# Token order 8p + n in the end stage, with the second channel half scaled and shifted by products on TensorE

## Chip, cores and metric

The kernel runs on one core of one Trainium2 chip. The metric is the device time of a launch in microseconds; the time of a kernel is the median of its runs. All data are fp32.

## The reference

A batch of 16 graphs with 1024 nodes (tokens) and 256 channels passes two layers. Each ends with a residual and a layernorm over the channels:

```
x1 = layernorm(x  + attention(x, adj, ...))                    # layer 0
h  = relu(batchnorm((A_hat @ x1) @ W1.T + b1))                 # layer 1, 512 features
o  = batchnorm(h @ W2.T + b2)        # per channel: o * scale + shift, over all 16 x 1024 tokens
y  = layernorm(x1 + o)
```

The second batchnorm needs statistics over all tokens of all graphs. Its scale and shift are thus known only when the last graph's product with W2 is done, and everything after that point is the end stage.

## The kernel before

The work has four stages. Attention takes the 16 graphs one after the other (until about 1440 us), with the normalised x1 of each graph stored to device memory. The second stage aggregates x1 with the adjacency and applies W1 (until about 2150 us). The third normalises h and applies W2 (until about 2350 us), leaving `o2T[b]`: for each graph b a tile of 128 channels x 2 halves x 1024 tokens, channels on the partitions. The fourth is the end stage.

The instructions of TensorE (PE), ScalarE (ACT) and VectorE (DVE) run in the order in which the program writes them; a scheduler doesn't move them. GpSimd (POOL) also runs in order. SyncE (SP) issues most transfers; the stores of x1 in attention are issued by POOL, in `finish_x1` and, for the last graph, in the second stage.

In memory a graph's x1 is kept as the tile lies on chip: `x1_d[b]` has for each partition p a run of 8 KB, which holds the tokens p, 128 + p, 256 + p and so on. It is written so, read so by `load_x1l` for the second stage, and read so by `load_x1` for the end stage. The output is in plain token order, so the store of `y` breaks into pieces of one token, 1 KB each.

The end stage works graph by graph, in a loop over b that runs `residual2(b)`, then `scale_shift(b + 3)`, then `finish(b - 1)`:

- `scale_shift(b)` applies the batchnorm's scale `sg2` and shift `sh2` to `o2T[b]` in place on ACT, one instruction for each half of 128 channels. Scale and shift are one value for each partition here.
- `residual2(b)` turns `o2T[b]` so that tokens lie on the partitions, in blocks of 128 tokens; two blocks (a "pair") share a bank of PSUM. Pairs 0 and 1 go to two banks `pf`, and DVE adds x1 (`xf[b]`) to them and takes statistics. Pairs 2 and 3 go to the two banks of `held[b]`; there PE itself adds x1, by a product with the identity (`add_x1`), and DVE only takes statistics. `coefficients` makes the layernorm's factors from these, on POOL for nearly all graphs.
- `finish(b)` applies the factors chunk by chunk (a chunk is 128 tokens x 256 channels). Four chunks come from the held banks, four from `xf[b]`. ACT takes six and DVE two; for every third graph ACT takes five and DVE three; for the last graph DVE takes six. The result overwrites `o2T[b]` and is stored by SP. Then a later graph's x1 is loaded.

For graph 0 the eight transposing products into the held banks are written as plain products with the identity, since x1 was put there before:

```
nc.tensor.matmul(
    dst, src, ident, start=(b > 0 and j == c == 0), stop=(b == 0),
    is_transpose=(b > 0), skip_group_check=True,
)
```

The pools of PSUM: two banks for `pf`, and three tiles of two banks for `held`. In attention, bursts of scores and outputs are written out in a fixed order, 16 bursts for each graph; the normalised x1 of the graph before is applied and stored in bursts 2 to 4, and the x of a later graph is loaded in burst 5, into the buffer that the store frees.

Of the kernel before, what the change touches and what calls it, by code (L numbers as in the profile page):

```python
# [10 lines left out]
F32 = mybir.dt.float32  # L11
I32 = mybir.dt.int32
AF = mybir.ActivationFunctionType
ALU = mybir.AluOpType
# [4 lines left out]
P = 128  # L19
# [496 lines left out]
def fast_path(  # L516
# [49 lines left out]
    def tile_o(name):  # L566
        return psum["o"].tile([P, HALF], F32, tag="o", name=name)

    x1_d = [dram.tile([P, NCH, C], F32, tag=f"x1_{b}", name=f"x1_{b}") for b in range(B)]
    c_d = [dram.tile([1, N], F32, tag=f"c_{b}", name=f"c_{b}") for b in range(B)]  # L570
    dinv_d = dram.tile([1, N], F32, tag="dinv", name="dinv")
    den_d = [dram.tile([H, HALF], F32, tag=f"den_{g}", name=f"den_{g}") for g in range(2 * B)]
# [160 lines left out]
    with (  # L733
# [432 lines left out]
        def finish_x1(b, ns=range(NCH)):  # L1166
            st[b]["ln"][1](ns)
            if NCH - 1 in ns:
                nc.gpsimd.dma_start(x1_d[b], st.pop(b)["x"])

        def run(fs, k):
            for f, a in fs[:k]:
# [105 lines left out]

        def load_x1l(b):
            x1l[b] = xp.tile([P, NCH, C], F32, tag="x", name=f"x1l_{b}")  # L1280
            nc.sync.dma_start(x1l[b], x1_d[b])

        agg = {}

# [225 lines left out]
    with (  # L1510
# [123 lines left out]
        for b in range(1, B):  # L1634
            if 1 < b < B - 1:
                load_x1l(b + 1)
                x1_sums(b + 1)
            elif b == B - 1:
                h0 = []
                for i in range(2):  # L1640
                    t = xp.tile([P, 2, N], F32, tag="x", name=f"hl_0_{i}")
                    nc.sync.dma_start(t, h_d[0][:, 2 * i : 2 * i + 2, :])
                    h0 += [t[:, 0, :], t[:, 1, :]]
            steps = aggregate(b)
            for i, step in enumerate(steps):
                step()
                if i == len(steps) - 1 and b < B - 1:
                    later = linear1(b)
                if b > 1 or i > 0:
                    run_linear(lin, 3 if b == 1 and i in (3, 5) else 2)  # L1650
                if b == 1 and i == 0:
                    last_apply()
                    nc.gpsimd.dma_start(x1_d[B - 1], x_last)
                    load_x1l(2)
                    x1_sums(2)
            lin = later
            if b == 1:
                denominators_range()
            if b == 2:
                denominators_good()  # L1660
# [39 lines left out]
    with tc.tile_pool(name="hl", bufs=4) as hl, tc.tile_pool(name="o2p", bufs=1) as o2p:  # L1700
# [5 lines left out]

        def load_x1(b, pool, tag):
            xf[b] = pool.tile([P, NCH, C], F32, tag=tag, name=f"xf_{b}")
            nc.sync.dma_start(xf[b], x1_d[b])

        coefficients2, sg2, sh2 = batchnorm(bn2_st, cols["g2"], cols["be2"], CC, "bn2", nc.vector)
        hs_of = {0: h0}
# [70 lines left out]
                bn2_st[:, c, 2 * b + half, :], o2T[b][:, c, half * HALF : (half + 1) * HALF]  # L1783
            )

        def scale_shift(b, cs=range(CC)):
            for c in cs:
                for hs in (H0, H1) if b == 0 else (slice(0, N),):
                    o = o2T[b][:, c, hs]
                    nc.scalar.activation(  # L1790
                        o, o, AF.Identity, bias=sh2[:, c : c + 1], scale=sg2[:, c : c + 1]
                    )

        load_h(1)
        rest = []
        for b in range(B):
# [63 lines left out]
            for c in range(CC):  # L1860
                last = b == B - 1 and c == CC - 1
                if b:
                    for k, hs in (
                        [(k, hs) for hs in (H0, H1) for k in range(HC)] if last
                        else [(k, hs) for k in range(HC) for hs in (H0, H1)]
                    ):
                        mm(c, k, hs)
                if last:
                    for hs in (H0, H1):
                        nc.scalar.activation(  # L1870
                            o2T[b][:, c, hs], half_ps(c, hs), AF.Identity,
                            bias=cols["b2"][:, c : c + 1],
                        )
                        if hs == H0:
                            scale_shift(0, (0,))
                else:
                    nc.vector.tensor_scalar(
                        o2T[b][:, c, :], pss[c], cols["b2"][:, c : c + 1], None, ALU.add
                    )
                for half, hs in enumerate((H0, H1)):  # L1880
                    nc.vector.bn_stats(bn2_st[:, c, 2 * b + half, :], o2T[b][:, c, hs])
                if b == B - 1:
                    coefficients2(c)
# [8 lines left out]
        with (  # L1892
# [5 lines left out]

            held = {}

            def add_x1(b, pair):
                if b not in held:
                    held[b] = ps_held.tile([P, N], F32, tag="held", name=f"held_{b}")
                nc.tensor.matmul(
                    held[b][:, (pair - 2) * HALF : (pair - 1) * HALF], ident,
                    xf[b][:, 2 * pair : 2 * pair + 2, :].rearrange("p n c -> p (n c)"),
                    start=(b == 0), stop=(b > 0), skip_group_check=True,
                )

            def residual2(b):  # L1910
                xt = xf[b]
                last = b == B - 1
                st = small.tile([P, NCH, 6], F32, tag="ln_st", name=f"st_l1_{b}")
                for pair in range(2):
                    pt = ps_sum.tile([P, HALF], F32, tag="sum", name=f"pf_{b}_{pair}")
                    for j in range(2):
                        n = 2 * pair + j
                        for c in range(CC):
                            nc.tensor.transpose(
                                pt[:, j * C + c * P : j * C + (c + 1) * P],  # L1920
                                o2T[b][:, c, n * P : (n + 1) * P], ident,
                            )
                    xs = xt[:, 2 * pair : 2 * pair + 2, :].rearrange("p n c -> p (n c)")
                    nc.vector.tensor_add(xs, pt, xs)
                    for n in (2 * pair, 2 * pair + 1):
                        nc.vector.bn_stats(st[:, n, :], xt[:, n, :])
                if last:
                    first = coefficients(b, st, M0, nc.vector)
                if b:
                    held[b] = ps_held.tile([P, N], F32, tag="held", name=f"held_{b}")  # L1930
                for pair in range(2, 4):
                    pt = held[b][:, (pair - 2) * HALF : (pair - 1) * HALF]
                    for j in range(2):
                        n = 2 * pair + j
                        for c in range(CC):
                            dst = pt[:, j * C + c * P : j * C + (c + 1) * P]
                            src = o2T[b][:, c, n * P : (n + 1) * P]
                            nc.tensor.matmul(
                                dst, src, ident, start=(b > 0 and j == c == 0), stop=(b == 0),
                                is_transpose=(b > 0), skip_group_check=True,  # L1940
                            )
                    if b:
                        add_x1(b, pair)
                for n in range(4, NCH):
                    nc.vector.bn_stats(st[:, n, :], held[b][:, (n - 4) * C : (n - 3) * C])
                if last:
# [21 lines left out]
            def finish(b, *coeffs):  # L1968
                xt, hx = xf.pop(b), held.pop(b)
                y = o2T[b].rearrange("p c n -> p (c n)").rearrange("p (n c) -> p n c", c=C)  # L1970
                last = b == B - 1
                third = b % 3 == 1
                for n in (0, 1, 2, 3, 6, 7) if last else (0, 1, 2) if third else (0, 1):
                    rstd, nmr = coeffs[n // 4]
                    nc.vector.tensor_scalar(
                        y[:, n, :], hx[:, (n - 4) * C : (n - 3) * C] if n >= 4 else xt[:, n, :],
                        rstd[:, n : n + 1], nmr[:, n : n + 1], ALU.mult, ALU.add,
                    )
                for n in (4, 5) if last else (4, 5, 6, 7, 3) if third else (4, 5, 6, 7, 2, 3):
                    rstd, nmr = coeffs[n // 4]  # L1980
                    nc.scalar.activation(
                        y[:, n, :], hx[:, (n - 4) * C : (n - 3) * C] if n >= 4 else xt[:, n, :],
                        AF.Identity, bias=nmr[:, n : n + 1], scale=rstd[:, n : n + 1],
                    )
                dst = out[b].rearrange("(n p) c -> p n c", p=P)
                if last:
                    nc.sync.dma_start(dst[:, M0, :], y[:, M0, :])
                    nc.scalar.dma_start(dst[:, 4:6, :], y[:, 4:6, :])
                    nc.sync.dma_start(dst[:, 6:8, :], y[:, 6:8, :])
                elif b >= B - 4:  # L1990
# [7 lines left out]
            add_x1(0, 2)  # L1998
            add_x1(0, 3)
            for b in range(1, 4):  # L2000
                scale_shift(b, (0,))
            for b in range(2):
                scale_shift(b, (1,))
            coeffs = {}
            for b in range(B):
                coeffs[b] = residual2(b)
                if b == 0:
                    scale_shift(2, (1,))
                    scale_shift(3, (1,))
                elif b + 3 < B:  # L2010
                    scale_shift(b + 3)
                if b:
                    finish(b - 1, *coeffs.pop(b - 1))
# [44 lines left out]
```

## Time and profile before

| | us |
|---|---|
| median of 3 runs (2448.04 to 2448.85) | 2448.72 |
| the profiled execution: its own time | 2446.23 |
| its span in the profile | 2444.4 |
| PE busy / DVE busy / ACT busy / POOL busy | 2399.5 / 1865.7 / 1234.9 / 476.4 |
| end stage, from the last product with W2 to the end of the span | about 2350 to 2444 |
| last activation starts / last store is issued | 2438.95 / 2439.54 |
| bytes moved by the DMA engines over the span | 221.97 MB, mean 91 GB/s |

The span is the time from the first to the last instruction that the profiler recorded on the core; the run's own time is 1.8 us longer. "Busy" is the sum over an engine's instructions. A matmul's length in the profile includes its drain, which overlaps the next one, so the distance between starts tells the rate. A plain fp32 product leaves two MATMUL records.

### The profile page before, as it was taken

How to read it: one execution, taken by the hardware profiler on the slowest of the kernel's cores; microseconds unless marked ns; L12 is line 12 of the kernel's file. 1: busy time of each engine (PE TensorE's matmuls, PEld its weight loads, DVE VectorE, ACT ScalarE, POOL GpSimd, SP SyncE). 2: the span in 40 equal slices, each digit the busy share in tenths (PEclk: the TensorE clock that was granted, in tenths of full speed). 3: DMA queues.
4: the chain of work that ended last, by engine and by line, in shares of the span. 5: the costliest groups of instructions: out<-in, count | busy, mean ns of one | idle time of the engine just before them, and what ended most of it. 6: DMA issues, size and time to landing. Idle time of an engine off the chain costs nothing.

```text
span 2444.4 us, 32579 instructions
## 1 busy us (share of the span) xinstructions
PE 2399.5 (98%) x12302; PEld 1011.3 (41%) x12302; DVE 1865.7 (76%) x2577; ACT 1234.9 (51%) x1538; POOL 476.4 (19%) x486
## 2 busy tenths in 40 slices
PE   9999999999999999999999999999999999999986
PEld 5343443443434434434344343344444444444443
DVE  5688878878888788788888888956556566479978
ACT  7376675765765756657647667421111111045567
POOL 0021112111311211122112112422122122010026
PEclk9999999999999999999999999999999999999998
DMA  5124232332231332322322327221222222165569
GB/s 164 40 41 86 57 49 70 70 53 67 39 83 53 49 84 56 53 70 54 65 61 44 83 49 96 83 103 69 96 94 77 95 86 86 69 239 174 172 215 337
DMA packets 423190, 221.97 MB, mean 91 GB/s; under 512 B 361584, under 2 KB 394864, under 8 KB 414576
## 3 DMA queue, kind: packets, MB, share of 16 engines
q1 hardware_dynamic: 417920, 169.20, 28.3%
q0 software_dynamic: 4832, 50.34, 4.9%
q8 instruction: 98, 1.61, 0.3%
q14 instruction: 68, 0.56, 0.1%
q10 hardware_dynamic: 272, 0.26, 0.0%
HBM read 136.06 MB, written 83.69 MB: 90 GB/s over the span
## 4 chain that ended last, share of the span: by engine, by line
PE 86%; DVE 9%; ACT 3%; DMA 1%; issue 1%; POOL 0%; POOLq 0%; DVEq 0%; ACTq 0%
PE ps L1051 18%; PE po L1072 18%; PE pgb L883 7%; PE b_agg L1556 4%; PE pga L883 4%; PE c_agg L1556 4%; PE pk L980 4%; PE b_o L1763 3%; PE pv L993 3%; PE a_agg L1556 2%; PE b_h L1588 2%; PE pgc L883 2%; PE pgd L883 2%; PE c_o L1763 2%; PE a_o L1763 2%; PE c_h L1588 2%
## 5 line engine op out<-in xcount | busy, mean ns | idle before, releaser
L1056 ACT ACTIVATE p<-ps 128x1024 f32<-128x1024 f32 x512 | 497.5, 1021 | 183.7 <-PE ps L1051 130.1
L1082 DVE TENSOR_TENSOR acc<-acc,p 128x1024 f32<-128x1024 f32 x384 | 500.1, 1302 | 54.2 <-ACT p L1056 29.3
L1051 PE MATMUL ps<-qT,kT 64*64 64x512 f32 x4096 | 488.1, 592 | 0.3 <-ACT p L1056 0.3
L1072 PE MATMUL po<-p,v 64*64 64x512 f32 x4096 | 485.3, 589 | 0.0
L1147 POOL TENSOR_TENSOR o<-o,r_all 128x512 f32<-128x512 f32 x62 | 94.8, 1538 | 1091.1 <-DVE r_all L1141 1014.5
L1072 PEld LDWEIGHTS po<-p,v 64*64 64x64 f32 x4096 | 158.1, 133 | 281.4 <-issue 274.4
L1051 PEld LDWEIGHTS ps<-qT,kT 64*64 64x64 f32 x4096 | 151.4, 133 | 286.9 <-issue 249.2
L834 DVE SCALAR_TENSOR_TENSOR wg<-wg,adj_s 128x1024 f32<-128x1024 f32 x128 | 149.5, 1216 | 16.5 <-ACT wg L830 16.5
L825 ACT ACTIVATE wg<-crow,ccol 128x1024 f32<-128x1024 f32 x128 | 146.8, 1147 | 0.4 <-DMA crow<-c 0.4
L830 ACT ACTIVATE wg<-wg 128x1024 f32<-128x1024 f32 x128 | 136.0, 1062 | 0.9
L980 PE MATMUL pk<-xT,kvw_s 128*128 128x512 f32 x256 | 121.9, 598 | 3.1 <-ACT drow L1126 3.1
L993 PE MATMUL pv<-kvw_s,xT 128*128 128x256 f32 x512 | 124.0, 385 | 0.0
L993 PEld LDWEIGHTS pv<-kvw_s,xT 128*128 128x128 f32 x512 | 94.9, 190 | 50.0 <-issue 13.4
L893 ACT ACTIVATE qT<-qT 128x512 f32<-128x512 f32 x60 | 37.1, 626 | 149.8 <-DVE qT L896 145.3
L883 PE MATMUL pgb<-wg,S 128*128 128x512 f32 x240 | 111.0, 605 | 0.0
L883 PE MATMUL pga<-wg,x 128*128 128x512 f32 x240 | 109.6, 599 | 0.7 <-ACT qT L906 0.7
L1556 PE MATMUL a_agg<-ahT,x1l 128*128 128x512 f32 x240 | 108.1, 593 | 0.7 <-ACT agg L1298 0.7
L1148 POOL TENSOR_TENSOR x<-x,o 128x512 f32<-128x512 f32 x62 | 107.7, 1748 | 2.4
L1556 PE MATMUL b_agg<-aT,x1S 128*128 128x512 f32 x240 | 107.9, 592 | 0.0
L654 ACT COPY p_agg<-a_agg 128x512 f32<-128x512 f32 x15 | 8.8, 587 | 183.4 <-PE a_agg L1556 183.4
L690 POOL TENSOR_TENSOR x1S<-x1l 128x512 f32<-128x512 f32 x15 | 18.9, 1263 | 352.3 <-PE c_agg L1556 349.0
L1080 DVE TENSOR_TENSOR acc<-p,p 128x1024 f32<-128x1024 f32 x64 | 77.3, 1208 | 7.5 <-ACT p L1056 7.5
(231 smaller groups left out, 3477.1 us busy)
## 6 DMA issues: line engine op xcount, KB each, us to landing
h<-hw POOLq DMA_DIRECT2D x16, 2048.0 KB, 6.7
hl<-h SPq DMA_DIRECT2D x32, 1024.0 KB
x<-x POOLq DMA_DIRECT2D x16, 1024.0 KB, 4.2
x1l<-x SPq DMA_DIRECT2D x16, 1024.0 KB
xf<-x SPq DMA_DIRECT2D x16, 1024.0 KB
o<-oS SPq DMA_DIRECT2D x62, 256.0 KB
o<-o SPq DMA_DIRECT2D x248, 64.0 KB
x<-in_x_dram SPq DMA_DIRECT2D x15, 1024.0 KB
```

The lines of the kernel that those rows point to most:

```text
L825: nc.scalar.activation(w, s["crow"], AF.Abs, bias=s["ccol"][:, n : n + 1])
L830: nc.scalar.activation(w, w, AF.Tanh, scale=0.5)
L834: nc.vector.scalar_tensor_tensor(w, w, 1.0, adj_s[:, n, :], op0=ALU.subtract, op1=ALU.mult)
L883: nc.tensor.matmul(ps, left, right, start=(start and i == 0), stop=(i == NCH // 2 - 1), skip_group_check=True,)
L980: nc.tensor.matmul(ps, kvw_s[:, c, kc * P : (kc + 1) * P], s["xT"][:, c, hs], start=(c == 0), stop=(c == CC - 1),)
L993: nc.tensor.matmul(pt[:, j * C : (j + 1) * C], s["xT"][:, c, n * P : (n + 1) * P], kvw_s[:, c, C : 2 * C], start=(c == 0), stop=(c == CC - 1),
L1051: nc.tensor.matmul(ps[kh * D : (kh + 1) * D, hd * HALF : (hd + 1) * HALF], kT[r, pr, ks], qT[r, pr, qh * HALF : (qh + 1) * HALF], start=Tr ...
L1056: nc.scalar.activation(p, ps, AF.Exp)
L1072: nc.tensor.matmul(g["po"][kh][hd * D : (hd + 1) * D, :], s["v"][r, m, h * D : (h + 1) * D], p[r, hd * HALF : (hd + 1) * HALF], start=(m = ...
L1082: nc.vector.tensor_add(g["acc"], g["acc"], p)
L1556: nc.tensor.matmul(ps, left, right, start=(start and i == 0), stop=(i == NCH // 2 - 1), skip_group_check=True,)
L1763: nc.tensor.matmul(ps, left, right, start=(start and i == 0), stop=(i == 1), skip_group_check=True,)
```

## The change

1. x1 is stored in plain token order: `x1_d[b]` is 1024 x 256. The store in attention and the load for the second stage go through the view `x1_chunks`, with pieces of 1 KB. The store is issued by ACT's queue where POOL issued it.
2. The end stage reads x1 through the view `x1_runs`: partition p holds the tokens 8p to 8p + 7, a run of 8 KB. The output is stored in the same way. The blocks of tokens for the turn are therefore every eighth column, `o2T[b][:, c, n::8]`.
3. ACT scales and shifts only the first 128 channels. For the second 128, the product that turns a block has the diagonal matrix of the scales (`side[:, 0]`) in the identity's place, and a further product of each bank adds the shift (`side[:, 1]` holds the shift of channel k in all columns of row k, and is multiplied with the identity, repeated for both blocks).
4. Order: `back_first` (first half's transposes, and for pairs 2 and 3 the addition of x1) and `back_second` (second half's products) replace the loops of transposes. For graph 0 all four `back_first` are issued ahead.
5. `finish` gives DVE one chunk and ACT seven; for the last graph four each. Where before the last four graphs' outputs were stored in parts, the last two are now, the last one as halves.

The core of the diff:

```diff
-    x1_d = [dram.tile([P, NCH, C], F32, tag=f"x1_{b}", name=f"x1_{b}") for b in range(B)]
+    x1_d = [dram.tile([N, C], F32, tag=f"x1_{b}", name=f"x1_{b}") for b in range(B)]
+    x1_chunks = [d.rearrange("(n p) c -> p n c", p=P) for d in x1_d]
+    x1_runs = [d.rearrange("(p n) c -> p n c", n=NCH) for d in x1_d]
...
-                nc.gpsimd.dma_start(x1_d[b], st.pop(b)["x"])
+                nc.scalar.dma_start(x1_chunks[b], st.pop(b)["x"])
...
-            nc.sync.dma_start(x1l[b], x1_d[b])
+            nc.sync.dma_start(x1l[b], x1_chunks[b])
...
-                    nc.gpsimd.dma_start(x1_d[B - 1], x_last)
+                    nc.scalar.dma_start(x1_chunks[B - 1], x_last)
...
-            nc.sync.dma_start(xf[b], x1_d[b])
+            nc.sync.dma_start(xf[b], x1_runs[b])
...
-        def scale_shift(b, cs=range(CC)):
...
+        def scale_shift(b):
+            o = o2T[b][:, 0, :]
+            nc.scalar.activation(o, o, AF.Identity, bias=sh2[:, 0:1], scale=sg2[:, 0:1])
+
+        side = o2p.tile([P, 2, P], F32, name="side")
...
+            def back_first(b, pair, ps):
+                for j in range(2):
+                    n = 2 * pair + j
+                    nc.tensor.matmul(
+                        ps[:, j * C : j * C + P], o2T[b][:, 0, n::NCH], ident,
+                        start=(j == 0), stop=False, is_transpose=True, skip_group_check=True,
+                    )
+                if pair > 1:
+                    nc.tensor.matmul(
+                        ps, ident, xf[b][:, 2 * pair : 2 * pair + 2, :].rearrange("p n c -> p (n c)"),
+                        start=False, stop=False, skip_group_check=True,
+                    )
+
+            def back_second(b, pair, ps):
+                for j in range(2):
+                    n = 2 * pair + j
+                    nc.tensor.matmul(
+                        ps[:, j * C + P : (j + 1) * C], o2T[b][:, 1, n::NCH], side[:, 0, :],
+                        start=False, stop=False, skip_group_check=True,
+                    )
                 nc.tensor.matmul(
+                    ps.rearrange("p (j c) -> p j c", j=2)[:, :, C1], side[:, 1, :],
+                    ident.unsqueeze(1).to_broadcast([P, 2, P]),
+                    start=False, stop=True, skip_group_check=True,
                 )
...
-                for n in (0, 1, 2, 3, 6, 7) if last else (0, 1, 2) if third else (0, 1):
+                for n in (0, 1, 2, 3) if last else (0,):
...
-                for n in (4, 5) if last else (4, 5, 6, 7, 3) if third else (4, 5, 6, 7, 2, 3):
+                for n in (4, 5, 6, 7) if last else (4, 5, 6, 7, 1, 2, 3):
...
-                dst = out[b].rearrange("(n p) c -> p n c", p=P)
+                dst = out[b].rearrange("(p n) c -> p n c", n=NCH)
...
+            nc.vector.tensor_scalar(side[:, 0, :], ident, sg2[:, 1:2], None, ALU.mult)
+            nc.vector.tensor_scalar(side[:, 1, :], ident, 0.0, sh2[:, 1:2], ALU.mult, ALU.add)
```

More of the change, by code (lines that the diff above doesn't have):

```diff
@@ L1784, in statistics2 @@
             )
-        def scale_shift(b, cs=range(CC)):
[L1787 to L1792, printed above, removed]
+        def scale_shift(b):
+            o = o2T[b][:, 0, :]
+            nc.scalar.activation(o, o, AF.Identity, bias=sh2[:, 0:1], scale=sg2[:, 0:1])
+        side = o2p.tile([P, 2, P], F32, name="side")
         load_h(1)
@@ L1874, in fast_path @@
                         if hs == H0:
-                            scale_shift(0, (0,))
+                            scale_shift(0)
                 else:
@@ L1899, in fast_path @@
             held = {}
-            def add_x1(b, pair):
-                if b not in held:
-                    held[b] = ps_held.tile([P, N], F32, tag="held", name=f"held_{b}")
+            def back_first(b, pair, ps):
[17 more added lines that the diff above has]
+                    )
                 nc.tensor.matmul(
-                    held[b][:, (pair - 2) * HALF : (pair - 1) * HALF], ident,
-                    xf[b][:, 2 * pair : 2 * pair + 2, :].rearrange("p n c -> p (n c)"),
-                    start=(b == 0), stop=(b > 0), skip_group_check=True,
+                    ps.rearrange("p (j c) -> p j c", j=2)[:, :, C1], side[:, 1, :],
+                    ident.unsqueeze(1).to_broadcast([P, 2, P]),
+                    start=False, stop=True, skip_group_check=True,
                 )
@@ L1913, in residual2 @@
                 st = small.tile([P, NCH, 6], F32, tag="ln_st", name=f"st_l1_{b}")
-                for pair in range(2):
[L1915 to L1922, printed above, removed]
+                pts = [ps_sum.tile([P, HALF], F32, tag="sum", name=f"pf_{b}_{pair}") for pair in range(2)]
+                held[b] = ps_held.tile([P, N], F32, tag="held", name=f"held_{b}")
+                pts += [held[b][:, H0], held[b][:, H1]]
+                if b == 0:
+                    for pair in range(4):
+                        back_first(b, pair, pts[pair])
+                for pair in range(2):
+                    pt = pts[pair]
+                    if b:
+                        back_first(b, pair, pt)
+                    back_second(b, pair, pt)
                     xs = xt[:, 2 * pair : 2 * pair + 2, :].rearrange("p n c -> p (n c)")
@@ L1928, in residual2 @@
                     first = coefficients(b, st, M0, nc.vector)
-                if b:
-                    held[b] = ps_held.tile([P, N], F32, tag="held", name=f"held_{b}")
                 for pair in range(2, 4):
[L1932 to L1941, printed above, removed]
                     if b:
-                        add_x1(b, pair)
+                        back_first(b, pair, pts[pair])
+                    back_second(b, pair, pts[pair])
                 for n in range(4, NCH):
@@ L1971, in finish @@
                 last = b == B - 1
-                third = b % 3 == 1
-                for n in (0, 1, 2, 3, 6, 7) if last else (0, 1, 2) if third else (0, 1):
+                for n in (0, 1, 2, 3) if last else (0,):
                     rstd, nmr = coeffs[n // 4]
                     nc.vector.tensor_scalar(
-                        y[:, n, :], hx[:, (n - 4) * C : (n - 3) * C] if n >= 4 else xt[:, n, :],
-                        rstd[:, n : n + 1], nmr[:, n : n + 1], ALU.mult, ALU.add,
+                        y[:, n, :], xt[:, n, :], rstd[:, n : n + 1], nmr[:, n : n + 1],
+                        ALU.mult, ALU.add,
                     )
-                for n in (4, 5) if last else (4, 5, 6, 7, 3) if third else (4, 5, 6, 7, 2, 3):
+                for n in (4, 5, 6, 7) if last else (4, 5, 6, 7, 1, 2, 3):
                     rstd, nmr = coeffs[n // 4]
@@ L1984, in finish @@
                     )
-                dst = out[b].rearrange("(n p) c -> p n c", p=P)
+                dst = out[b].rearrange("(p n) c -> p n c", n=NCH)
                 if last:
                     nc.sync.dma_start(dst[:, M0, :], y[:, M0, :])
-                    nc.scalar.dma_start(dst[:, 4:6, :], y[:, 4:6, :])
-                    nc.sync.dma_start(dst[:, 6:8, :], y[:, 6:8, :])
-                elif b >= B - 4:
+                    nc.scalar.dma_start(dst[:, M1, :], y[:, M1, :])
+                elif b >= B - 2:
                     nc.sync.dma_start(dst[:, M1, :], y[:, M1, :])
@@ L1996, in finish @@
                     load_x1(b + 7, *((hl, "hl") if 3 <= b < 7 else (xp, "x")))
-            add_x1(0, 2)
-            add_x1(0, 3)
             for b in range(1, 4):
-                scale_shift(b, (0,))
-            for b in range(2):
-                scale_shift(b, (1,))
+                scale_shift(b)
+            nc.vector.tensor_scalar(side[:, 0, :], ident, sg2[:, 1:2], None, ALU.mult)
+            nc.vector.tensor_scalar(side[:, 1, :], ident, 0.0, sh2[:, 1:2], ALU.mult, ALU.add)
             coeffs = {}
@@ L2006, in fast_path @@
                 coeffs[b] = residual2(b)
[L2007 to L2010, printed above, removed]
+                if b and b + 3 < B:
                     scale_shift(b + 3)
```

## The prediction

> **What bounds the kernel now.** I read the page first: TensorE (PE) holds 86% of the chain that ended last, and the 40 slices show it saturated until the last two. The changed end stage lies in those two, so I cut that stretch (the answer of busy time by stretch; columns: stretch, its length, then busy us and instructions of PE, PEld, DVE, ACT and POOL, granted clock, DMA share, GB/s).
>
> ```profile
> 2385.00:2390.00 5.00, 3.85 (x21) 2.32 (x20) 4.93 (x14) 5.00 (x9) 3.72 (x11) 1.00 1.06 393
> 2400.00:2405.00 5.00, 3.86 (x21) 2.32 (x20) 4.93 (x13) 5.00 (x9) 3.72 (x12) 1.00 1.05 403
> 2425.00:2430.00 5.00, 3.51 (x19) 1.92 (x17) 4.93 (x15) 3.17 (x7) 3.87 (x11) 1.00 0.75 257
> ```
>
> Here VectorE (DVE) and ScalarE (ACT) are both full, the DMA engines too, and PE has slack. The waits of 2350 to 2445 us say who holds whom:
>
> ```profile
> PEld pf L1919 <- DVE xf L1924: 27.8, 28, 1.2
> PE pf L1919 <- DVE xf L1924: 12.0, 19, 0.7
> POOL w_l L1956 <- DVE st_l L1945: 9.0, 12, 1.8
> ACT o L1981 <- POOL w_l L1965: 8.7, 6, 2.5
> ```
>
> No row of PE, DVE or ACT waits for a DMA: the full DMA engines are nobody's releaser. PE waits for DVE to empty the `pf` banks. The chain in order of time (start, length, what) gives one batch:
>
> ```profile
> 2390.20 0.61 DVE xf L1924
> ...
> 2390.83 0.75 DVE st_l L1926 x2
> 2391.59 0.60 DVE xf L1924
> ...
> 2392.55 0.41 DVE st_l L1926
> 2392.96 1.33 DVE st_l L1945 x4
> 2394.29 0.64 DVE o L1975 x2
> 2394.93 0.61 DVE xf L1924
> ```
>
> From add to add: 4.73 us with two applied chunks; with three, 5.05. From batch 1's first add (2361.18) to batch 14's (2423.95) the mean is 62.77 / 13 = 4.83 us. ACT needs about as much: by the timeline two scale-and-shift start 2.27 us before what follows, four chunks from PSUM take 1.79, two from SBUF 0.99, so 5.05.
>
> PE's prices, from the timeline (start, length with drain, what). Starts, not lengths, give the rate:
>
> ```profile
> 50.86 1.89 PE L993 MATMUL pv<-kvw_s,xT 128*128 128x256 f32 x8
> 52.59 1.88 PE L980 MATMUL pk<-xT,kvw_s 128*128 128x512 f32 x4
> 2356.18 1.95 PE L1938 MATMUL held<-ident,o 128*128 128x128 f32 x16
> 2363.71 0.60 PE L1938 MATMUL held<-ident,o 128*128 128x128 f32 x4
> 2364.15 1.02 PE L1904 MATMUL held<-xf,ident 128*128 128x512 f32 x2
> 2365.01 0.60 PE L1938 MATMUL held<-ident,o 128*128 128x128 f32 x4
> ```
>
> The third row is batch 0, where eight transposing products are written as plain products: 16 records, two for each product, while a true transpose (fourth row, four of them) leaves one. So per record: 128 columns 0.11 us (0.44 / 4 for transposes; (1.95 - 0.27) / 15 = 0.112 for plain ones), 256 columns 1.73 / 8 = 0.216, 512 columns 0.86 / 2 = 0.43. A transpose costs 0.11, a plain 128-column product 0.22, a 256-column one 0.43, a 512-column one 0.86. PE today: 16 transposes and two 512-column adds of x1 per batch, 1.76 + 1.72 = 3.5 us of the 4.83.
>
> **What the Trainium skill says.** "FP8 and Floating Point Precision", TensorE Precision Notes: a true fp32 product takes four passes. "TensorE: Matmul & The Clock Gate", Wait — 56ns, not 53.3ns?: 128 columns take about 56 ns a pass and 512 about 216 when warm. The trace agrees: 0.86 us is four times 216 ns, and the transpose's 0.11 is two passes. "SBUF — State Buffer", Door 1: The DMA port swizzle, has a note on 16-byte lines: an access that crosses to a new line each time pays a penalty, of no stated size. No instruction of PE in this trace reads at such a stride, so nothing here shows it.
>
> **The change part by part.**
>
> *PE, end stage.* Per batch it removes the 8 transposes of channels 128 to 255, and adds 8 plain products with `side` (each 128 columns, 0.22 to 0.23) and 4 shift products (one for each bank, 256 columns, 0.43). Kept: 8 transposes, and two x1 adds. Sum: 8 x 0.11 + 8 x 0.224 + 4 x 0.43 + 2 x 0.86 = 0.88 + 1.79 + 1.72 + 1.72 = 6.1 us. That is 2.6 us more than PE now does and 1.3 more than the present 4.83 us period. PE becomes the bound of the stage.
>
> *DVE and ACT.* DVE applies one chunk a batch in place of two or three: 4.73 - 0.32 = 4.41 us. ACT loses one scale-and-shift (1.14) and applies seven chunks: 1.14 + 1.79 + 3 x 0.49 = 4.4. Both then lie under PE's 6.1, so their relief is worth nothing; its cover is PE. Building `side` is two small DVE instructions (about 0.25 us each, between the 0.15 of the one-column row and the 0.40 of L1975) after the last coefficient, done near 2354.9.
>
> *Start.* Now PE waits till 2355.36 for ACT to scale batch 0's second half. Afterwards it needs only `side`; batch 0's transposes and x1 adds (2.6 us) run before, in PE's idle 2352 to 2355. Start about 2355.05, 0.3 us earlier. Batch 0 then has 4 x (0.45 + 0.43) = 3.5 us of PE left, and 15 batches x 6.1 = 91.7 follow: PE's last bank is full at 2450.3.
>
> *Tail.* The four statistics of the held banks wait for both banks, 1.45 us; coefficients on DVE 1.0 (2434.32 to 2435.31 today); POOL's power and two products 1.9; then ACT alone applies four chunks, 2.0 with the handover, and issues at about +6.6 us. Today ACT's issue at 2439.54 is followed by 4.9 us to the end; the last transfer grows from 256 KB to 512 KB but has the queues to itself. End of span: 2450.3 + 0.1 + 6.6 + 4.9 = 2461.9 against 2444.4, **+17.5 us**.
>
> *Output in 8 KB runs.* Stretches with stores alone moved 341 GB/s (310 at a share of 0.91 from 2435 to 2440); the large x1 and h stores of POOL's queue took 4.9% of the span for 50.34 MB, which is 420. So 16.8 MB of output need some 40 us of DMA time for 49. Worth 0: nobody waits for it, and PE at 6.1 us a batch slows the demand further. Final loads of x1 keep 8 KB runs.
>
> *x1 stores on ACT's queue, in 1 KB runs; x1l loads in 1 KB runs.* POOL loses 16 issues of 0.645 us; ACT gains 16 of about 0.43 (its one store today), each behind a wait for its own activations and for an earlier transfer's semaphore. What is queued behind is the relu of qT and the exponentials, and PE waits for those; but from 60 to 1500 us PE waited 0.3 us for L1056 and 0.7 for L906, and ACT sat 117 us waiting for PE's scores. I take 0; bounds: -1 (POOL is freed) and +7 (no issue hidden). SP waits at L755 for the store to land before it loads the next x (13 times); the loaded x is first used three of a batch's sixteen bursts later (about 16 us of some 86), so 0. The x1l loads take some 0.6 us more each, under aggregates of about 43 us.
>
> *Strided weights.* `o2T[..., n::8]` reads one fp32 in 32 bytes. 0 if the load keeps its rate. Upper bound by my estimate (the page gives no size): a load at half rate, 0.21 for 0.107 us. Five of six strided loads in a `pf` bank and four in a held bank have no longer product to hide behind: 18 x 0.105 = 1.9 us a batch, 8.0 in all; end 30 us later still. I take 0: transposing loads last 140 ns and plain ones 191 for the same bytes, so the plain load is not at the limit of reading, and two thirds of the strided loads are plain.
>
> The sum is against the profiled execution: span 2444.4, its own time 2446.23. The median of the three runs lies 2.5 above that, so I add to the median: 2448.7 + 17.5 = **2466**.
>
> **The rivals.**
> 1. PE bound, strided loads at the old rate: 2466, own range 2462 to 2471 (step of 6.0 to 6.3 us). Chance 0.60.
> 2. PE bound, strided loads at half rate: +47, so 2496. For: the skill's note. Against: the margin just named. Chance 0.28; something between or a cost in attention on top, 0.06.
> 3. Faster: PE hides. If a product with `side` cost one record of 0.11 and the shift one of 0.216, PE would need 0.9 + 0.9 + 0.9 + 1.7 = 4.4, level with DVE and ACT; then DVE's 20 fewer chunks x 0.32 give -6.4: 2442. It decides at a PE batch of 4.8 us. Against it stand the 16 records of batch 0. Chance 0.04.
> 4. It doesn't do what it says, for instance runs that stay short: no transfer is waited for, so it changes none of these. Without effect at all: 0.02.
>
> **How the numbers follow.** About 0.2% (5 us) can be told from no change. Faster: 0.04. Same: 0.03 (rival 4 and a piece of 3). Slower: the rest, 0.93. The range takes rival 1 from 2461 and reaches through rival 2 to 2498.
>
> **What would show it.** Right: in the changed profile PE is full from 2355 to 2450, the wait of `pf` for DVE is gone, DVE and ACT wait for PE and are busy some 70%; first transposes of successive batches lie 6.1 us apart; the products with `side` leave two records each; outputs show 8 KB packets and a DMA share well under 1. The strided case shows as weight loads of `o` over 0.2 us. Wrong: DVE still without a gap in the loop, or PE waits for ACT in attention.

## The result, and the profile after

| | median, us | runs |
|---|---|---|
| before | 2448.25 | 6 (2446.53 to 2448.85) |
| after | 2492.08 | 6 (2491.85 to 2492.80) |

The ratio is 1.018, with a 95% interval of 1.0167 to 1.0193: 44 us slower. The profiled execution of the changed kernel has a span of 2491.0 us against 2444.4, so 46.6 us are to be found in the trace.

All but 1.0 us of them lie in the end stage. From 60 to 1500 us PE is busy for 1435.90 of 1440 us in both kernels, and the last product with W2 starts 1.0 us later after the change. That 1.0 us isn't the change's: the eight records of `pv` that begin at 8.63 us, long before the first changed instruction, took 2.86 us up to the next product where they took 1.85 before. From that next product to the last one with W2, all 14 traces of this case take 2339.3 to 2339.4 us.

For the end stage, first the same three stretches that were shown of before (stretch, its length, then busy us and instructions of PE, PEld, DVE, ACT and POOL, granted clock, DMA share, GB/s):

```profile
2385.00:2390.00 5.00, 5.00 (x24) 4.51 (x25) 4.32 (x11) 2.00 (x3) 3.29 (x9) 1.00 0.64 218
2400.00:2405.00 5.00, 5.00 (x26) 4.49 (x24) 4.34 (x11) 2.73 (x5) 2.59 (x8) 1.00 0.67 261
2425.00:2430.00 5.00, 5.00 (x25) 4.35 (x25) 3.65 (x9) 1.67 (x3) 3.46 (x10) 1.00 0.67 233
```

PE has no gap at the full clock, DVE and ACT have, and the DMA share has fallen from 1.06, 1.05 and 0.75 to about 0.65. But the PEld column has almost doubled as well, from 2.3 to 4.5 us, while PE's count of instructions rose only from 21 to some 25. The waits of 2350 to 2491 us (who waits for whom; total, times, longest) have turned round:

```profile
ACT o L1988 <- POOL w_l L1973: 63.6, 16, 9.3
POOL w_l L1964 <- DVE st_l L1953: 55.3, 14, 4.5
DVE st_l L1953 <- PE held L1921: 47.1, 16, 3.2
```

Read from the bottom: DVE waits for PE's last product into a held bank, POOL for DVE's statistics, ACT for POOL's factors. Before, `pf` on PE waited for DVE; that row is gone. The chain in order of time (start, length without drain, what) is now PE alone, and its lengths are PE's prices. A `pf` bank and then a held bank:

```profile
2400.48 0.22 PE pf L1904 x2
2400.70 0.95 PE pf L1917 x4
2401.64 0.43 PE pf L1921 x2
...
2403.68 0.22 PE held L1904 x2
2403.90 0.86 PE held L1909 x2
2404.76 0.82 PE held L1917 x4
```

Transposes (L1904), the addition of x1 (L1909) and the shift (L1921) cost what the prediction gave them: 0.22 for two, 0.86 and 0.43. The four records of the products with `side` (L1917) do not: 0.95 and 0.82 us in place of 4 x 0.112 = 0.45. For each MATMUL record the profile has one of a weight load (PEld; 12550 of each), which takes one operand, the weights, into PE; in L1904 and L1917 that is the block of `o`. A transpose has a transposing load, any other product a plain one. These loads tell which part is long. Grouped by tile from 2365 to 2470 us (busy us, mean ns of one), and last a transposing load of the kernel before, from 2365 to 2430 us:

```profile
L1917 PEld LDWEIGHTS held<-side,o 128*128 128x128 f32 x110 | 30.4, 324 | 9.9 <-issue 6.7
L1917 PEld LDWEIGHTS pf<-side,o 128*128 128x128 f32 x104 | 26.7, 329 | 0.0
L1904 PEld LDWEIGHTS held<-ident,o 128*128 128x128 f32 x54 | 10.1, 188 | 1.4
...
L1921 PEld LDWEIGHTS held<-ident,side 128*128 128x128 f32 x54 | 8.7, 199 | 0.0
```

```profile
L1938 PEld LDWEIGHTS held<-ident,o 128*128 128x128 f32 x107 | 13.0, 142 | 7.1 <-issue 7.1
```

After the change L1917 and L1904 load blocks of the same `o` tiles with the same step of eight elements; L1921 loads plain weights without a step. The plain loads with a step take 324 to 329 ns against 199 without; the transposing ones take 188 (142 in the kernel before), and it costs them nothing, since two still follow each other in 0.22 us. The difference of a `pf` and a held bank fits loads: in a held bank the first of the four is loaded under the long x1 product before it (loads from 2404.16 us, the products from 2404.76). The excess is 0.50 us for the four of a `pf` bank (0.126 each) and 0.37 for the three exposed ones of a held bank (0.124 each).

### The profile page after: what moved, and what is told of

The parts are those of the page before. It is cut to its first block, busy times and chain, and to the rows that moved or that the text cites. A ratio compares the mean times of both kernels' runs of the same rounds, so it can differ in the third digit from the quotient of the medians.

```text
span 2491.0 us, 32995 instructions
## 1 busy us (share of the span) xinstructions
PE 2464.1 (99%) x12550; PEld 1084.9 (44%) x12550; DVE 1861.8 (75%) x2557; ACT 1229.2 (49%) x1542; POOL 463.8 (19%) x470
## 4 chain that ended last, share of the span: by engine, by line
PE 89%; DVE 7%; ACT 2%; DMA 1%; issue 0%; POOL 0%; POOLq 0%; DVEq 0%
PE ps L1053 18%; PE po L1074 18%; PE pgb L885 6%; PE b_agg L1558 4%; PE pga L885 4%; PE c_agg L1558 4%; PE pk L982 4%; PE b_o L1765 3%; PE pv L995 3%; PE a_agg L1558 2%; PE b_h L1590 2%; PE pgd L885 2%; PE pgc L885 2%; PE a_o L1765 2%; PE c_o L1765 2%; PE c_h L1590 2%
```

## The experiments

Two theories remain. **S**: the end stage goes at PE's pace, and the excess is the eight-element step of the plain weights. **The rivals**: the excess belongs to the other half of the change, the order 8p + n with its 8 KB runs and queues, or to the step of the transposes too, or PE is not what paces the stage. The expectations spell them out for each run; what they call a batch is one graph. All times are medians; before was 2446.6 to 2447.0 in the runs beside these. Each diff shows the lines on which its run turns; `...` marks lines left out.

**1 and 2. The step taken away**, with every DMA as in the changed kernel. Run 1 takes it from both halves, which is the diff; run 2 has only its second pair of lines, the products with `side`. Tokens then lie in another order than x1 and the output, so these two runs are for their times:

```diff
-                        ps[:, j * C : j * C + P], o2T[b][:, 0, n::NCH], ident,
+                        ps[:, j * C : j * C + P], o2T[b][:, 0, n * P : (n + 1) * P], ident,
...
-                        ps[:, j * C + P : (j + 1) * C], o2T[b][:, 1, n::NCH], side[:, 0, :],
+                        ps[:, j * C + P : (j + 1) * C], o2T[b][:, 1, n * P : (n + 1) * P], side[:, 0, :],
```

> The changed kernel, but both halves of o2T are read as weights in blocks of 128 neighbouring tokens (step of one fp32) in place of every eighth; all else is the same, so the blocks' tokens no longer match the x1 that is added and the place they are stored to. Theory S (the 32-byte step slows the loads of plain products): a record of a product with side falls from about 0.24 us to 0.112, a batch from 7.87 us to 6.1, and the run from 2492 us to 2492 - 15 x 1.75 - 1.7 = about 2464. Rival P (a product with side costs 0.24 us a record whatever the step, since it changes its weights each time): no change, 2492.

> The changed kernel, but only the products with side (second channel half) read o2T at a step of one fp32; the transposes of the first half keep the step of 32 bytes (again the tokens of the second half then don't match). Theory S with transposes that keep their rate (two still start 0.22 us apart from the next): the same as with both at unit step, about 2464. If the transposes' loads are slowed too and this was only hidden: between, 2466 to 2472. Rival P: 2492.

Measured: 2463.97 us (1.0068 of before, 1.0051 to 1.0085) and 2464.50 (1.0071, 1.0054 to 1.0087). The timeline of the second (start, length with drain, what), one `pf` bank and the start of the next:

```profile
2401.53 0.38 PE L1904 MATMUL pf<-ident,o 128*128 128x128 f32 x2
2401.75 0.61 PE L1917 MATMUL pf<-side,o 128*128 128x128 f32 x4
2402.20 0.60 PE L1921 MATMUL pf<-ident,side 128*128 128x256 f32 x2
2402.63 0.38 PE L1904 MATMUL pf<-ident,o 128*128 128x128 f32 x2
```

From start to start the transposes, still with the step, take 0.22 us, and the four product records 0.45: the forecast's prices. The plain loads are back at 192 ns (run 1, 2365 to 2450 us):

```profile
L1917 PEld LDWEIGHTS pf<-side,o 128*128 128x128 f32 x112 | 14.7, 192 | 0.0
```

The step under the products alone is worth some 28 us. Under the transposes it is worth 0.5 us at most: their loads take 187 ns in run 2 and 142 in run 1, and the two times differ by no more than that.

**3 and 4. Each half of the change alone.** Run 3 has the new order of tokens, the runs of 8 KB and ACT's queue, with all transposes and ACT's scale and shift as before; graph 0 is turned like the others. Run 4 keeps the old order, stores and queues, and makes the second 128 channels by products at unit step.

Run 3, against the kernel before:

```diff
-                                o2T[b][:, c, n * P : (n + 1) * P], ident,
+                                o2T[b][:, c, n::NCH], ident,
...
-                            src = o2T[b][:, c, n * P : (n + 1) * P]
+                            src = o2T[b][:, c, n::NCH]
```

Run 4, against the changed kernel:

```diff
-                        ps[:, j * C + P : (j + 1) * C], o2T[b][:, 1, n::NCH], side[:, 0, :],
+                        ps[:, j * C + P : (j + 1) * C], o2T[b][:, 1, n * P : (n + 1) * P], side[:, 0, :],
...
-                dst = out[b].rearrange("(p n) c -> p n c", n=NCH)
+                dst = out[b].rearrange("(n p) c -> p n c", p=P)
```

> The token order 8p + n alone: x1 and output in 8 KB runs, both channel halves turned by transposes at a step of 32 bytes, scale and shift of both halves on ACT and the chunks split between DVE and ACT as before (graph 0 is turned like the others). PE needs 16 x 0.11 + 1.72 = 3.5 us a batch if transposes keep their rate at this step, so DVE and ACT set the pace as before: 2447 to 2451 (the start is some 1 us later, since graph 0's x1 is added after its transposes). If transposes at that step cost 0.24 us each: 5.6 us a batch, 2462. If the relief of the DMA engines is worth something: below 2446.

> The products with side and the shift products alone: x1 and output laid out and issued as before (8 KB runs of x1, 1 KB runs of output, POOL's stores), all of o2T read at unit step. Theory S with PE as the bound: as the changed kernel with unit step, 2463 to 2466, since a batch on PE is 6.1 us and the DMA engines need some 5.2 us for a batch's load and store. If the DMA engines bind once they carry 1 KB stores beside the loads: later than that by 3 us or more. Rival P: 2490 or more.

Measured: the layout alone 2450.32 (1.0013, 1.0006 to 1.0020); the products alone 2464.74 (1.0071, 1.0054 to 1.0088). The second equals runs 1 and 2 within 0.8 us, so beside products the new runs and queues are worth nothing in either direction. The first lies inside its expected span, but not for the reason given there. It keeps the old pace in its loop (4.72 us from one graph's first addition to the next, 4.73 before); what it lost, it lost at the start of the stage, where graph 1's first addition comes at 2364.55 us instead of 2361.18, 3.4 later and not 1. Its stretch of 2355 to 2360 us, and PE's timeline there:

```profile
2355.00:2360.00 5.00, 3.80 (x13) 2.97 (x14) 2.79 (x6) 5.00 (x6) 0.00 (x0) 0.50 0.26 108
```

```profile
2351.40 0.38 PE L1921 MATMUL pf<-ident,o 128*128 128x128 f32 x1 [0.78 <-ACT o L1872]
2356.20 1.76 PE L1921 MATMUL pf<-ident,o 128*128 128x128 f32 x7 [4.42 <-ACT o L1792]
...
2358.61 1.91 PE L1906 MATMUL held<-xf,ident 128*128 128x512 f32 x2
```

Here graph 0's x1 is added behind its transposes, as for the other graphs, so PE has nothing to do while ACT scales. A block of every eighth token also needs both halves of the tile scaled, one instruction of ACT more than before (0.7 us). PE waits 4.42 us and starts 0.84 us later than before, at half the full clock (0.50, the mean of the stretch): two records of x1 take 1.70 us from start to start where they take 0.86, and graph 0 takes PE 5.67 us where the prices sum to 3.5.

**5. Is it that clock?** Run 3, with graph 0's two x1 additions issued ahead as a filler; their result is then overwritten.

```diff
+            for pair in (2, 3):
+                nc.tensor.matmul(
+                    held[0][:, (pair - 2) * HALF : (pair - 1) * HALF], ident,
+                    xf[0][:, 2 * pair : 2 * pair + 2, :].rearrange("p n c -> p (n c)"),
+                    start=True, stop=True, skip_group_check=True,
+                )
```

> The token order alone, as run before, but PE multiplies graph 0's x1 by the identity right after its last product with W2, as the kernel before does (the result is overwritten by the transposes later, so it only fills PE's wait for ACT). Theory C (in the layout-alone run PE stood idle from 2351 to 2356 us, and its granted clock fell to a half for graph 0): the 3.4 us come back but for the x1 products that now run twice (1.7 us, of which DVE's lag hides some): about 2447 to 2449. Rival: the 3.4 us come from the strided transposes or from x1's place after them: stays at 2450 to 2451.

Measured: 2449.11 (1.0009, 1.0000 to 1.0018), between the two expectations. PE's wait shrank to 3.75 us and the mean clock of that stretch rose to 0.70, but its timeline shows that the low clock was still there:

```profile
2355.89 1.04 PE L1921 MATMUL pf<-ident,o 128*128 128x128 f32 x7 [3.75 <-ACT o L1792]
2356.77 0.83 PE L1940 MATMUL held<-ident,o 128*128 128x128 f32 x4
2357.39 1.92 PE L1906 MATMUL held<-xf,ident 128*128 128x512 f32 x2
2359.10 1.06 PE L1940 MATMUL held<-ident,o 128*128 128x128 f32 x4
```

The seven transposes take 0.88 us, near the full rate, but the two records of x1 take 1.71 again, and graph 0 takes 5.16 us in place of 5.67. So the run didn't take the low clock away and is no clean test of it: by these sums graph 0 still loses 1.7 us on PE, after 2.2 in run 3, and how much of the 3.4 us the clock explains stays open.

**6 and 7. Where does the step begin to cost?** The order of tokens is made 2p + i in groups of 256 (a step of two elements, 8 bytes, runs of 2 KB) and 4p + i in groups of 512 (four elements, 16 bytes, runs of 4 KB). For the second:

```diff
+            def block(n):
+                first = n // 4 * 4 * P + n % 4
+                return slice(first, first + (P - 1) * 4 + 1, 4)
...
-                        ps[:, j * C + P : (j + 1) * C], o2T[b][:, 1, n::NCH], side[:, 0, :],
+                        ps[:, j * C + P : (j + 1) * C], o2T[b][:, 1, block(n)], side[:, 0, :],
```

> The changed kernel with token order 2p + i inside blocks of 256 tokens: weights are read at a step of 8 bytes, x1 and output move in runs of 2 KB. Theory L (16-byte lines: with two values used of each line the plain load keeps its rate): 2464 as at unit step, a record of a product with side at 0.112 us. Rival G (the cost grows with the step): between, about 2470 to 2478, records of 0.13 to 0.18 us.

> The changed kernel with token order 4p + i inside blocks of 512 tokens: weights are read at a step of 16 bytes, runs of 4 KB. Theory L (one value of each 16-byte line is already the worst case): 2492 as at 32 bytes, records of 0.24 us, plain loads of 0.32 us. If a step of four fp32 is still free, as the skill's page counts it: 2464. Rival G: about 2478 to 2485.

Measured: step 2 2465.77 (1.0073, 1.0056 to 1.0090), step 4 2491.26 (1.0178, 1.0161 to 1.0195). Weight loads of the products, step 2 and then step 4:

```profile
L1921 PEld LDWEIGHTS pf<-side,o 128*128 128x128 f32 x112 | 15.6, 198 | 0.0
```

```profile
L1921 PEld LDWEIGHTS pf<-side,o 128*128 128x128 f32 x106 | 26.8, 324 | 0.0
```

198 ns and 324 ns: next to nothing at two elements, the whole price at four. At two, four product records take 0.46 to 0.47 us where they took 0.45, and the run lies 1.3 to 1.8 us above runs 1 and 2. Between four and eight there is no further loss. The Trainium skill, "SBUF — State Buffer", Door 1: The DMA port swizzle, says both that a 16-byte line needs at least two hits for full bandwidth and that fp32 can be strided up to four for free. For the plain loads the runs agree with the first (two fp32 of each line are used at step 2, one at step 4), which is theory L of the expectations, and not with the second; the measurement decides. That the line itself is the reason is not shown: only the steps 1, 2, 4 and 8 were run, and the transposing loads, which took 142 ns at unit step, take 196 already at step 2, for two of them still in 0.23 us.

**8 and 9. Without the shift.** Of 6.1 us a graph on PE, 1.72 are shift products. Run 8 is run 4 without them, run 9 the same with the order 2p + i. Both leave out the shift of the second 128 channels.

```diff
-                nc.tensor.matmul(
-                    ps.rearrange("p (j c) -> p j c", j=2)[:, :, C1], side[:, 1, :],
-                    ident.unsqueeze(1).to_broadcast([P, 2, P]),
-                    start=False, stop=True, skip_group_check=True,
-                )
```

> Products with side at unit step in the layout of the kernel before, without the shift products, so the shift of the second 128 channels is left out. If PE's sum bounds the stage: a batch on PE falls by 4 x 0.43 to 4.4 us, level with DVE's 4.41 and ACT's 4.4, so the loop of 15 batches ends 15 x 1.7 = 25 us earlier than with products alone (2464.7): 2439 to 2443, faster than before. If the DMA engines bind at 1 KB stores (some 5.2 us for a batch's load and store while loads last): 2444 to 2449. If the shift products were hidden: 2464.

> Products with side at a step of 8 bytes, without the shift products (the shift of the second 128 channels is left out), stores in runs of 2 KB; otherwise as the unit-step run without shift. That run's engines were done at about 2432 us and its stores ended at 2440. If the 1 KB stores held it up (rival: only the last batch's own chain did): 2437 to 2440, 3 to 5 us less than 2442.6. If not: 2442 to 2443.

Measured: 2442.55 (0.9979, 0.9970 to 0.9988) and 2441.76 (0.9979, 0.9970 to 0.9987). PE's sum falls to 4.4 us a graph, and from 2360 to 2420 us, in run 8, PE and DVE are full together (PE's lengths include drains):

```profile
2360.00:2420.00 60.00, 59.57 (x378) 46.38 (x378) 58.93 (x155) 54.28 (x100) 45.09 (x130) 1.00 0.91 335
```

So the relief of DVE and ACT is real, 4.5 to 4.9 us, once PE doesn't cover it. Longer runs of the store, with the step of two, changed this by less than 1 us.

**10 and 11. A cheaper shift.** The shift as one bf16 product of three rows (the fp32 value split in three), and transposes with ACT's scale and shift in every fourth graph; run 10 with the order of before, run 11 with 2p + i.

```diff
+                    nc.tensor.matmul(
+                        ps.rearrange("p (j c) -> p j c", j=2)[:, :, C1], ones3[:3, :],
+                        shift3[:3, :].unsqueeze(1).to_broadcast([3, 2, P]),
+                        start=False, stop=True, skip_group_check=True,
+                    )
```

> A version meant to beat both: the layout of the kernel before (1 KB stores), products with side at unit step for three graphs of four and transposes with ACT's scale and shift for the fourth; the shift product from graph 2 on as one bf16 product of three rows (the shift split into three bf16 parts, repeated ones as weights). PE then needs 1.7 us less 0.4 for shifts: 4.8 us for a graph by product and 3.5 for one by transposes, 4.5 on average; DVE 4.49 and ACT 4.55. If the engines bound it: 15 x (4.83 - 4.53) = 4.5 us less than before, 2441 to 2444. If the DMA engines bind with 1 KB stores, as the full share at the end of the run without shift hints: 2443 to 2446.

> The same mixture with token order 2p + i, so weights at a step of 8 bytes and stores in runs of 2 KB, x1's stores on ACT's queue. If the DMA engines bind the mixture with 1 KB runs: 1 to 3 us less than that run, 2440 to 2443. If not: equal to it within 1 us. Against the kernel before: 2441 to 2444, faster by about 0.15 to 0.25%.

Measured: 2451.45 (1.0020, 1.0012 to 1.0027) and 2455.72 (1.0036, 1.0022 to 1.0049): both expectations missed. PE is busy for all of 2365 to 2425 us in both, so it still sets the pace. Run 10's timeline shows why:

```profile
2404.29 0.61 PE L1942 MATMUL pf<-side,o 128*128 128x128 f32 x4
2404.83 0.28 PE L1947 MATMUL pf<-shift,ones 3*128 3x256 bf16 x1
2405.04 0.44 PE L1915 MATMUL pf<-ident,o 128*128 128x128 f32 x2
2405.32 0.61 PE L1942 MATMUL pf<-side,o 128*128 128x128 f32 x4
```

From start to start, the four product records before the bf16 one take 0.54 us where they took 0.44 to 0.45, the bf16 one 0.21, and the two transposes after it 0.28 where they took 0.22. Together that is 0.37 us for the shift against 0.43 in fp32; the expectation had put 0.1 (0.4 for a graph's four banks). Whether the type or the form of three rows makes the neighbours longer was not separated. Run 11's `pf` bank is dearer still, 1.12 us against 1.03, with two transposes at 0.34: beside the bf16 product the step of two came with 4.3 us more, and what makes it so was not separated either, since the runs and the queue changed with it.

**12. Products in two graphs of five**, fp32 shift, unit step, order of before; DVE's share of the chunks is 1, 2 or 3 by the kind of graph.

```diff
+        def by_product(b):
+            return b % 5 in (0, 2)
...
+                k = 1 if by_product(b) else 3 if b % 5 == 4 else 2
```

> The order of tokens, the stores and the queues of the kernel before; in two of every five graphs of the end stage the second 128 channels come from products at unit step with an fp32 shift product, in the other three from transposes with the scale and shift on ScalarE, and VectorE's share of the chunks is shifted between the kinds of graph to level it. Theory S (a product graph takes TensorE 6.1 us, a graph of transposes 3.5; VectorE and ScalarE about 4.66 on average where they took 4.83): TensorE needs 0.4 x 6.1 + 0.6 x 3.5 = 4.54 us, so VectorE and ScalarE stay the bound and 15 x 0.17 = 2.6 us are saved: 2443.5 to 2445.5 against about 2446.8 for the kernel before. Rival: the buffers are too shallow to even out the two kinds of graph, each graph goes at its own slower engine, and the time is 2447 or more.

Measured: 2445.17 against 2446.63 (0.9992, 0.9984 to 1.0001): inside the span expected, and not told apart from no change. From 2365 to 2425 us PE is busy 59.17 of 60 us (drains included), DVE 58.69 and ACT 56.80, so all three are level, and the waits of 2365 to 2430 us show what is left:

```profile
POOL w_l L1983 <- DVE st_l L1972: 9.8, 14, 1.8
PEld pf L1909 <- DVE xf L1962: 7.0, 16, 0.6
```

PE waits for DVE again, but for 7.7 us (0.7 on PE's own row) where the two rows had 36.9 in the kernel before over the same stretch: there is hardly slack left to give away. Of the versions that compute the whole reference it has the lowest time, by 1.5 us, and the interval reaches from 0.2 us slower to 3.9 faster.

## Why the prediction was wrong

**The bound: right.** PE became the bound, the wait of `pf` for DVE disappeared, and DVE and ACT wait. The sign of the forecast and this part of its mechanism hold, and runs 1, 2 and 4, where the step is gone from the products, measured its number: 17.0 to 17.8 us slower than before, with 17.5 predicted. With the step it was 43.8.

**The step that failed: "Strided weights ... I take 0".** The term 8 x 0.224 = 1.79 us for the products with `side` measured 2 x 0.95 + 2 x 0.82 = 3.54. The reason given for 0, that plain loads take longer than transposing ones for the same bytes and so are "not at the limit of reading", failed: with the step it is the plain load that becomes long (192 to 324 ns) and holds up PE, while the transposing load, though it also lengthens (142 to 188), costs nothing. The length of a load at unit step did not tell its length at a step of eight. Rival 2, which had the weights at half rate, 2496 and a chance of 0.28, was the case, in place but not in detail: it counted 18 exposed loads of both kinds at 0.105 each (1.9 us); it is 14 plain ones, four in a `pf` bank and three in a held one, at about 0.125 (1.75). That the two sums come out so near is luck: too many loads were counted, each at too little.

**The sum, with that term put right.** PE ended at 2450.3 by the prediction and at 2479.15 in the trace, 28.9 later:

- 0.6: the products of graph 0 start at 2355.65, not 2355.05. 1.0 us was already there from the launch's first 12 us, and `side` was ready 0.4 sooner than put.
- 1.8: graph 0 takes 5.3 us, not 3.5. The products of its four banks take 1.05, 0.84, 0.85 and 0.85 us in place of 0.45 each.
- 26.5: fifteen graphs at 118.18 / 15 = 7.88 us (2360.97 to 2479.15), not 6.11.

ACT's store was issued 6.5 us after PE's end (6.6 predicted), and the end came 5.3 us later (4.9). 17.5 + 28.9 + 0.3 is 46.7 with these roundings, and 46.6 was measured.

**Costed at nothing, and rightly.** The output in 8 KB runs: from 2360 us on, 3905 packets were moved where there were 18032, and runs 1 and 2, with the new runs and queues, lie within 0.8 us of run 4, with the old ones. The x1 stores on ACT's queue: ACT's issues take 0.37 us, PE is as busy in attention as before, and the stretch up to the last product with W2 is as long in every trace (2339.3 to 2339.4 us). DVE and ACT "busy some 70%" was put for a PE period of 6.1; at 7.9 they were busy 64.2 and 57.6 of the 110 us from 2360 to 2470.

**Rival 3, the gain**, had its place right (PE at 4.4 us a graph, level with DVE and ACT), and its size in part: it put 6.4 us, and run 8, which is that case, gained 4.5. But its mechanism, one record for a product with `side`, was not: each leaves two, and run 8 gets to 4.4 us only by leaving out the shift.

## What to carry to other kernels

Before work is moved to an engine with slack, multiply out what it takes there: a graph of 16 transposes and two additions took PE 3.5 us, and the move cost 2.6 more against 1.3 of slack. Then look at how each operand is read: plain fp32 weights with a step of two elements loaded here at nearly the full rate, and with four or eight a record took up to 0.24 us in place of 0.11. So a layout that lengthens DMA runs by striding the weights could be had here up to a step of two, at 1.3 to 1.8 us between fp32 products; whether it is as cheap beside bf16 products is open (run 11, with other changes too, was 4.3 us slower than run 10). The DMA queue that was full but that nobody waited for gave nothing back when it was relieved.

## What the runs showed of the hardware that was not expected

- Only plain loads paid for the step: at eight elements two fp32 transposes still took 0.22 us, four plain records up to 0.95.
- Transposing loads lengthen already at a step of two (196 ns, 142 at unit step, 188 at eight), and between fp32 products this cost at most 0.01 us for two transposes.
- The cost of the step jumps and hardly slopes: 2464.0 to 2464.7 us at one element, 2465.8 at two, 2491.3 at four, 2492.1 at eight.
- The granted clock, as a mean over 2355 to 2360 us, was 1.00 where PE had waited 3.04 us (before), 0.70 after 3.75 (run 5) and 0.50 after 4.42 (run 3). The Trainium skill, "TensorE: Matmul & The Clock Gate", What's actually happening, puts an idle window at about 3.4 us; the three runs agree with it. They differ also in what follows the wait (plain products before, transposes in runs 3 and 5), so the wait is not shown to be the only reason.
- One bf16 product of three rows between fp32 ones went with longer neighbours: 0.37 us in all, of which 0.21 is its own.
- The first products of a launch vary: the first eight `pv` records, at some 8.6 us, took 1.8 to 2.9 us from one trace to another, and everything up to the end stage moved with them. What makes them vary was not looked into.
